# A weight column in 12 to 14 vector operations instead of 17, and another order of the opening work of a group-norm convolution

## The chip, the cores and the metric

One core of one Trainium2 chip. The metric is device time in microseconds (us) of one execution; medians of several executions are quoted, with the lowest and the highest. A traced execution also has a span, which is some 1.7 us shorter than its time (1101.58 against 1099.8 in the one traced run of the kernel before).

## The reference, cut to what matters

```python
x = x + conv(group_norm(x), quantise(U))       # x: 160 images of 128 channels, 32x32, fp32

# group norm: 32 groups of 4 channels; mean and variance over (4, 32, 32)
# the convolution: 5 weight sets, set n for images n*32 .. n*32+31 of the kernel's order;
#   3x3, 128 -> 128 channels, padding 1
s1 = (max(U) - min(U)) / 3                     # over ALL five sets
v1 = s1 * floor(U / s1)
s2 = s1 / 5
v2 = s2 * floor((U - v1) / s2)
w  = v1 + v2
```

Two things follow for the start. No weight can be quantised before all five sets have been read and reduced to one maximum and one minimum. And with k1 and k2 for the two floors, w = s2 * (5*k1 + k2): the bracket is a small integer, exact in half precision, so the kernel puts only the integers into TensorE's weights and multiplies s2 into the normalised image.

## The kernel before: the parts that matter

A column is one of the three columns of the 3x3 stencil: 128x128x3 weights, read with a stride of 3 elements. It takes seven VectorE instructions for each floor, and 17 in all:

```python
def floor_div(self, k, v, n, t, parts):
    r, nr, hi, lo = parts                     # 1/s, -1/s, s in two parts
    yield nc.vector.tensor_scalar(n, v, r, ROUND, ALU.mult, ALU.add)      # round by adding a
    yield nc.vector.tensor_scalar_add(n, n, -ROUND)                       # large constant
    yield nc.vector.scalar_tensor_tensor(t, n, hi, v, ALU.mult, ALU.subtract)
    yield nc.vector.scalar_tensor_tensor(t, n, lo, t, ALU.mult, ALU.add)
    yield nc.vector.scalar_tensor_tensor(t, t, nr, n, ALU.mult, ALU.add)
    yield nc.vector.tensor_tensor(t, t, n, ALU.is_lt)
    yield nc.vector.tensor_sub(k, n, t)

def quantise(self, pool, un, name, combine):
    ...
    yield from self.floor_div(k1, un, nn, tt, self.parts1)
    yield nc.vector.tensor_scalar_mul(v1, k1, self.s1)
    yield nc.vector.tensor_sub(rest, un, v1)
    yield from self.floor_div(k2, rest, nn, tt, self.parts2)
    yield combine(k1, k2, v1)                 # in make_column: m = 5*k1 + k2
```

`make_column` then transposes the column on TensorE and takes it out of PSUM (TensorE's result memory) on ScalarE (`wt`). Each image is normalised by ScalarE (`z`) and split into a half-precision high part (`hi`, ScalarE) and a low part (`lo`, VectorE). Images 0 to 2 are convolved directly: for each column six 128x512 products with the high part and six with the low part, accumulated in PSUM. From image 3 on the low part goes through combined rows (`conv`, with `d` and `st`).

In the traces here every engine's instructions come in the order in which the program issues them (e3 below moves one small product, and what stood behind it starts 5.9 us sooner), so the text below is read as the order of the work on each engine. The opening:

```python
chain = self.steps.from_range(spread)         # s1, s2, reciprocals, shrink: small VectorE steps
column = self.make_column(0, 1)
...                                           # chain and column 1 interleaved
measure(0, 1)                                 # sums and squares of images 0, 1 on ScalarE
self.stats[0].means(); self.stats[0].deviations(); self.stats[0].variances()
measure(2, 3)
self.stats[0].scales()
self.stats[1].means()
self.normalise(0); self.high_part(0)
self.stats[1].deviations(); self.stats[1].variances()
self.normalise(1); self.high_part(1)
self.stats[1].scales()
run(column)                                   # transposes, wt
self.low_part(0); self.low_part(1)
self.normalise(2); self.high_part(2)
self.normalise(3); self.high_part(3)
self.conv_direct(0, 1); self.conv_direct(1, 1)
column = self.make_column(0, 0)               # the second column: begun here
take(column, 5); self.low_part(2); measure(4, 5)
run(column); measure(6, 7)
self.conv_direct(2, 1); self.conv_direct(0, 0)
self.stats[2].means(); self.stats[2].deviations()
...
run(self.make_column(0, 2))                   # the third column
for i in range(self.imgs):
    for st in ready: st.means()               # small TensorE products for images 8 and up,
    for st in middle: st.variances()          # ahead of image i's products
    if i < self.FIRST: self.conv_direct(i, 2) # FIRST = 3
    else: self.conv(i)
    ...
```

A group's statistics take a chain over the engines: sums (ScalarE), `mv` (POOL), `means` (a small product on TensorE over the four channels), `ngm` (ScalarE), `dv` (POOL), `variances` (TensorE), `ve` (copied by ScalarE, then worked on by POOL with `shrink`), `rstd` and `shift` (POOL), and only then `z`.

## Time and profile before

| | value |
|---|---|
| time | 1100.32 us median of 3 (1100.0 to 1101.24) |
| span of the traced run (1101.58 us) | 1099.8 us |
| first product of image 0 | 34.41 us |
| first product of image 3 | 74.07 us |
| first product of image 4 | 83.55 us |
| image 4 to the end | 1016.25 us |

From image 4 on TensorE never waits, so the whole question is what happens in the first 84 us. The prediction below shows the lines. To read them: a line of the timeline gives start, duration, engine, line of the program, operation, operands; the bracket at its end is the engine's idle time before it and what ended that. A wait line gives total us, times, longest.

One more line matters when two traces are compared. VectorE reduces the weights as they arrive, and the first of the 128x1152 reductions waits for a transfer; from there eight of them run without a gap and the scales follow. Before:

```profile
7.42 1.35 DVE L381 TENSOR_REDUCE ext<-u 128x1 f32<-128x1152 f32 x1 [0.89 <-DMA u<-in_L_conv_U_dram]
```

This moment differs from trace to trace (6.98 to 8.89 us in the nine of this study) with the landing of that transfer; the kernels e3 and e4, which are alike up to image 3, have it at 8.21 and 7.57. Where I write "from the landing", times are counted from it.

### The profile page before, as it was taken

How to read it: one execution, taken by the hardware profiler on the slowest of the kernel's cores; microseconds unless marked ns; L12 is line 12 of the kernel's file. 1: busy time of each engine (PE TensorE's matmuls, PEld its weight loads, DVE VectorE, ACT ScalarE, POOL GpSimd, SP SyncE). 2: the span in 40 equal slices, each digit the busy share in tenths (PEclk: the TensorE clock that was granted, in tenths of full speed). 3: DMA queues.
4: the chain of work that ended last, by engine and by line, in shares of the span. 5: the costliest groups of instructions: out<-in, count | busy, mean ns of one | idle time of the engine just before them, and what ended most of it. 6: DMA issues, size and time to landing. Idle time of an engine off the chain costs nothing.

```text
span 1099.8 us, 16007 instructions
## 1 busy us (share of the span) xinstructions
PE 1051.8 (96%) x5901; PEld 577.6 (53%) x5901; DVE 903.9 (82%) x1518; ACT 772.9 (70%) x1043; POOL 389.4 (35%) x716
## 2 busy tenths in 40 slices
PE   1689999999999999999999999999999999999997
PEld 0235555555555555555555555555555555555554
DVE  7868998897797989878889897797989877777774
ACT  4767977768776777777777768776778777776541
POOL 3423443342334343424353443334343423232210
PEclk9889999999999999999999999999999999999999
DMA  9506889889897989998979988888999898985664
GB/s 360 205 1 182 231 227 257 250 233 249 229 260 200 262 255 259 243 262 228 264 191 283 252 240 243 232 238 222 246 274 261 231 246 232 254 231 144 169 165 159
DMA packets 65462, 252.05 MB, mean 229 GB/s; under 512 B 3936, under 2 KB 3936, under 8 KB 65376
## 3 DMA queue, kind: packets, MB, share of 16 engines
q1 hardware_dynamic: 43344, 170.73, 42.1%
q0 software_dynamic: 22032, 80.23, 38.9%
q8 instruction: 48, 0.79, 0.3%
q14 instruction: 38, 0.31, 0.1%
HBM read 86.84 MB, written 83.89 MB: 155 GB/s over the span
## 4 chain that ended last, share of the span: by engine, by line
PE 94%; DVE 3%; DMA 1%; POOL 0%; ACT 0%; issue 0%; SPq 0%; DVEq 0%
PE eo L499 55%; PE eo L526 19%; PE m L526 19%; PE m L499 1%; DMA u<-in_L_conv_U_dram 1%; DVE ext L381 0%; DVE ext L382 0%; DVE xt L588 0%; DVE lo L465 0%; PE pg L211 0%; PE pt L415 0%; ACT z L452 0%; PE pg L196 0%; ACT hi L460 0%; POOL rstd L219 0%
## 5 line engine op out<-in xcount | busy, mean ns | idle before, releaser
L499 PE MATMUL eo<-hi,wt 128*128 128x512 f16 (+1 forms) x2862 | 686.8, 376 | 1.2 <-ACT wt L417 1.2
L499 PEld LDWEIGHTS <-wt 128*128 128x128 f16 x2934 | 288.7, 99 | 278.2 <-issue 8.3
L526 PEld LDWEIGHTS <-wt 128*128 128x128 f16 x2826 | 276.9, 99 | 196.0 <-issue 3.7
L552 ACT ACTIVATE mm<-m 128x1024 f16<-128x1024 f32 x157 | 160.0, 1019 | 233.4 <-PE m L526 233.4
L526 PE MATMUL eo<-d,wt 128*128 128x256 f16 (+1 forms) x1884 | 283.7, 273 | 0.0
L526 PE MATMUL m<-st,wt 128*128 128x512 f16 x942 | 230.4, 381 | 1.9 <-DVE xt L588 1.9
L452 ACT ACTIVATE z<-xt,shift,rstd 128x1024 f32<-128x1024 f32 x160 | 197.6, 1235 | 37.9 <-POOL shift L222 37.9
L465 DVE TENSOR_TENSOR lo<-z,hi 128x1024 f16<-128x1024 f32 x160 | 194.6, 1217 | 8.6 <-ACT hi L460 8.4
L581 DVE SCALAR_TENSOR_TENSOR sum<-pq,eo 128x1024 f32<-128x1024 f16 x153 | 185.9, 1215 | 16.0 <-PE eo L526 15.8
L190 POOL TENSOR_SCALAR mv<-squares 128x1 f32<-128x1 f32 x122 | 67.4, 553 | 313.8 <-ACT junk L187 311.3
L561 DVE TENSOR_TENSOR pq<-mm 128x512 f16<-128x512 f16 x157 | 66.4, 423 | 133.5 <-ACT mm L552 132.3
L594 POOL DMA_DIRECT2D xt<-sum x153 | 136.6, 894 | 85.4 <-DVE sum L581 69.5
L460 ACT CAST hi<-z 128x1024 f16<-128x1024 f32 x160 | 166.0, 1037 | 0.1
L187 ACT ACTIVATE junk<-xt,minus 128x1024 f16<-128x1024 f32 x122 | 140.5, 1152 | 2.5 <-POOL minus L180 1.5
L178 ACT ACTIVATE junk<-xt 128x1024 f16<-128x1024 f32 x122 | 127.7, 1047 | 11.3 <-DMA xt<-in_x_dram 11.1
L479 DVE TENSOR_TENSOR d<-lo 128x1024 f16<-128x1024 f16 x157 | 109.1, 695 | 5.4
L180 POOL TENSOR_SCALAR minus<-total 128x1 f32<-128x1 f32 x122 | 42.0, 345 | 107.1 <-ACT junk L178 106.3
L481 DVE TENSOR_TENSOR st<-lo 128x512 f16<-128x512 f16 x157 | 65.7, 419 | 0.0
L562 DVE TENSOR_TENSOR pq<-mm 128x512 f16<-128x512 f16 x157 | 65.5, 417 | 0.0
L482 DVE TENSOR_TENSOR st<-lo 128x512 f16<-128x512 f16 x157 | 65.4, 417 | 0.0
L171 DVE BATCH_NORM_STATS2 st<-xt 128x6 f32<-128x512 f32 x76 | 48.6, 680 | 0.0
L181 POOL TENSOR_SCALAR mv<-total 128x1 f32<-128x1 f32 x122 | 44.4, 364 | 0.1
(88 smaller groups left out, 416.1 us busy)
## 6 DMA issues: line engine op xcount, KB each, us to landing
xt<-in_x_dram SPq DMA_DIRECT2D x39, 2048.0 KB, 13.5
out_dram<-xt SPq DMA_DIRECT2D x39, 2048.0 KB, 7.4
xt<-sum POOLq DMA_DIRECT2D x153, 512.0 KB, 8.0
u<-in_L_conv_U_dram SPq DMA_DIRECT2D x4, 576.0 KB, 7.2
xt<-in_x_dram SPq DMA_DIRECT2D x4, 512.0 KB, 9.7
out_dram<-xt SPq DMA_DIRECT2D x3, 512.0 KB, 3.1
u<-in_L_conv_U_dram SPq DMA_DIRECT2D x2, 288.0 KB, 3.1
out_dram<-xt SPq DMA_DIRECT2D x2, 256.0 KB, 4.0
```

The source lines that it names most:

```text
L178: nc.scalar.activation(junk, image, ACTF.Copy, accum_out=total)
L187: nc.scalar.activation(junk, image, ACTF.Square, bias=self.minus[j], accum_out=squares)
L190: nc.gpsimd.tensor_scalar_mul(self.mv[:, j, 1:2], squares, 1.0 / image.shape[1])
L452: nc.scalar.activation(z, self.image(i), ACTF.Identity, bias=st.shift[:, j : j + 1], scale=st.rstd[:, j : j + 1],)
L460: self.nc.scalar.copy(hi.rearrange("p h w -> p (h w)"), self.z[i])
L465: self.nc.vector.tensor_sub(lo[:, 1 : self.H + 1, :].rearrange("p h w -> p (h w)"), self.z.pop(i), self.hi[i].rearrange("p h w -> p (h w)"),)
L479: nc.vector.tensor_sub(d, lo[:, 0:H, :], lo[:, 2 : H + 2, :])
L499: nc.tensor.matmul(target[:, h, r0 - h0 : r1 - h0, c0:c1], self.wts[n, col][:, k, :], tile[:, s0 : s0 + r1 - r0, c0 + dw : c1 + dw], start ...
L526: nc.tensor.matmul(target[:, :, c0:c1], self.wts[n, col][:, kind, :], source[:, :, c0 + dw : c1 + dw], start=start, stop=stop,)
L552: self.nc.scalar.mul(m, self.m.pop(i).rearrange("p a i w -> p a (i w)"), UP)
L581: nc.vector.scalar_tensor_tensor(self.sum[i], self.m.pop(i), 0.5 / UP, eo, ALU.mult, ALU.add)
L594: self.nc.gpsimd.dma_start(self.image(i), self.sum.pop(i), accum_op=ALU.add)
```

## The change

The intent: shorten what VectorE has to do for a column, and reorder the opening so that no engine waits for what another could have done earlier. A column takes 13 VectorE instructions, 12 where ScalarE does the first rounding (the second and third column), and 14 from image set 1 on. Cut to its core:

```diff
+    def nearest(self, pool, v, parts, name, by_scalar=False):
+        dt = mybir.dt.int16 if by_scalar else I32       # a conversion in place of ROUND
+        engine = self.nc.scalar.mul if by_scalar else self.nc.vector.tensor_scalar_mul
+        engine(n, v, parts[0])
     def floor_div(...):
-        yield nc.vector.tensor_scalar(n, v, r, ROUND, ALU.mult, ALU.add)
-        yield nc.vector.tensor_scalar_add(n, n, -ROUND)
-        yield nc.vector.scalar_tensor_tensor(t, n, hi, v, ALU.mult, ALU.subtract)
+        yield nc.vector.scalar_tensor_tensor(t, n, hi, v, ALU.mult, ALU.add)   # hi, lo of -s
     def quantise(...):
-        yield nc.vector.tensor_scalar_mul(v1, k1, self.s1)
-        yield nc.vector.tensor_sub(rest, un, v1)
+        yield nc.vector.scalar_tensor_tensor(rest, k1, self.parts1[1], un, ALU.mult, ALU.add)
     def make_column(self, n, col, by_scalar=False):
-        ... m = k1 * 5 + k2 on VectorE, 3 transposes
+        if n == 0: parts = ((k1, self.ident5), (k2, self.ident))     # merged on TensorE:
+        else: (m as before) parts = ((m, self.ident),)               # 5*I and I, in fp32 PSUM
@@ the opening @@
+        measure(0, 0, 1); measure(1, 0, 1)              # measure(stage, *images)
+        self.stats[0].means(); self.stats[0].deviations()
+        measure(0, 2, 3)
+        self.stats[0].variances(); self.stats[0].scales()
+        take(second, 1)                                 # ScalarE rounds the second column
+        measure(1, 2, 3)
+        self.stats[1].means(); self.stats[1].deviations()
+        parts(0)                                        # z and hi of image 0
+        self.stats[1].variances(); self.stats[1].scales()
+        self.normalise(1)
+        run(first)                                      # transposes, wt of the first column
+        self.high_part(1); parts(2)
+        take(second, 2); self.low_part(0)               # second column between the low parts
+        take(second, 2); self.low_part(1)
+        take(second, 2); self.low_part(2)
+        for part in (self.direct_hi, self.direct_lo):   # high parts of all three, then low
+            for i in range(self.FIRST): part(i, self.COLS[0])
+        measure(0, 4, 5); take(third, 1); measure(1, 4); run(second); measure(1, 5)
+        parts(3); measure(0, 6, 7)
+        ...                                             # products of the second column
+        run(third); measure(1, 6, 7); self.low_part(3); self.combinations(3)
@@ the loop, i < 3 @@
-                self.conv_direct(i, 2)
+                j = (i - 1) % self.FIRST                # the third column: images 2, 0, 1
+                self.direct_hi(j, self.COLS[2]); self.direct_lo(j, self.COLS[2])
+                (at i = 0 the means and deviations, at i = 1 the variances and scales of group 2)
+                self.residual(j)
```

More of the change, by code (lines that the diff above doesn't have):

```diff
@@ L31 @@
 WIDEST = 40.0
-ROUND = 12582912.0
 class Steps:
@@ L42, in __init__ @@
         self.parts1, self.parts2 = (
-            tuple(self.col(tag + part) for part in ("r", "nr", "hi", "lo"))
+            tuple(self.col(tag + part) for part in ("r", "n", "nhi", "nlo"))
             for tag in ("s1", "s2")
@@ L64, in parts @@
         def parts(out, s):
-            r, nr, hi, lo = out
+            r, neg, hi, lo = out
             yield nc.vector.reciprocal(r, s)
+            yield nc.vector.tensor_scalar_mul(neg, s, -1.0)
             yield nc.vector.tensor_single_scalar(
-                hi.bitcast(I32), s.bitcast(I32), -4096, op=ALU.bitwise_and
+                hi.bitcast(I32), neg.bitcast(I32), -4096, op=ALU.bitwise_and
             )
-            yield nc.vector.tensor_sub(lo, s, hi)
-            yield nc.vector.tensor_scalar_mul(nr, r, -1.0)
+            yield nc.vector.tensor_sub(lo, neg, hi)
         span = col("span")
@@ L97, in choose @@
         nc.vector.tensor_copy(self.far, far)
+    def nearest(self, pool, v, parts, name, by_scalar=False):
+        tag = "ns" if by_scalar else "nn"
+        dt = mybir.dt.int16 if by_scalar else I32
+        n = pool.tile(list(v.shape), dt, tag=tag, name=f"{tag}_{name}")
+        engine = self.nc.scalar.mul if by_scalar else self.nc.vector.tensor_scalar_mul
+        engine(n, v, parts[0])
+        return n
     def floor_div(self, k, v, n, t, parts):
         nc = self.nc
-        r, nr, hi, lo = parts
@@ L105, in floor_div @@
-        yield nc.vector.tensor_scalar(n, v, r, ROUND, ALU.mult, ALU.add)
-        yield nc.vector.tensor_scalar_add(n, n, -ROUND)
-        yield nc.vector.scalar_tensor_tensor(t, n, hi, v, ALU.mult, ALU.subtract)
+        r, _, hi, lo = parts
+        yield nc.vector.scalar_tensor_tensor(t, n, hi, v, ALU.mult, ALU.add)
         yield nc.vector.scalar_tensor_tensor(t, n, lo, t, ALU.mult, ALU.add)
-        yield nc.vector.scalar_tensor_tensor(t, t, nr, n, ALU.mult, ALU.add)
+        yield nc.vector.scalar_tensor_tensor(t, t, r, n, ALU.mult, ALU.add)
@@ L110, in floor_div, with quantise @@
         yield nc.vector.tensor_tensor(t, t, n, ALU.is_lt)
         yield nc.vector.tensor_sub(k, n, t)
-    def quantise(self, pool, un, name, combine):
-        nc = self.nc
-        nn, tt, k1, k2, v1, rest = (
-            pool.tile(list(un.shape), F32, tag=tag, name=f"{tag}_{name}")
-            for tag in ("nn", "tt", "k1", "k2", "v1", "rest")
+    def quantise(self, pool, un, name, dt, by_scalar=False):
+        yield (nn := self.nearest(pool, un, self.parts1, name, by_scalar))
+        tt, k1, k2, rest = (
+            pool.tile(list(un.shape), kind, tag=tag, name=f"{tag}_{name}")
+            for tag, kind in (("tt", F32), ("k1", dt), ("k2", dt), ("rest", F32))
@@ L120, in quantise @@
         )
         yield from self.floor_div(k1, un, nn, tt, self.parts1)
-        yield nc.vector.tensor_scalar_mul(v1, k1, self.s1)
-        yield nc.vector.tensor_sub(rest, un, v1)
+        yield self.nc.vector.scalar_tensor_tensor(
+            rest, k1, self.parts1[1], un, ALU.mult, ALU.add
+        )
+        yield (nn := self.nearest(pool, rest, self.parts2, name + "_2"))
         yield from self.floor_div(k2, rest, nn, tt, self.parts2)
-        yield combine(k1, k2, v1)
+        return k1, k2
@@ L128, in run @@
 def run(steps):
-    for _ in steps:
-        pass
+    while True:
+        try:
+            next(steps)
+        except StopIteration as end:
+            return end.value
 def group_mean_matrix(nc, pool):
@@ L247, in general_path @@
             wn = one.tile([P, C, TAPS], F32, tag="w", name=f"g_w{n}")
-            def combine(k1, k2, v1, wn=wn):
-                return nc.vector.scalar_tensor_tensor(
-                    wn, k2, steps.s2, v1, ALU.mult, ALU.add
-                )
-            run(steps.quantise(one, un, f"g{n}", combine))
+            k1, k2 = run(steps.quantise(one, un, f"g{n}", F32))
+            nc.vector.tensor_scalar_mul(wn, k1, steps.s1)
+            nc.vector.scalar_tensor_tensor(wn, k2, steps.s2, wn, ALU.mult, ALU.add)
             wt = one.tile([P, TAPS, C], F32, tag="wt", name=f"g_wt{n}")
@@ L399, in over_partitions, with make_column @@
         return spread
-    def make_column(self, n, col):
+    def make_column(self, n, col, by_scalar=False):
         nc, P = self.nc, self.P
-        m = self.qpool.tile([P, P, ROW], MM, tag="m", name=f"m{n}_{col}")
-        def combine(k1, k2, v1):
-            return nc.vector.scalar_tensor_tensor(m, k1, 5.0, k2, ALU.mult, ALU.add)
         un = self.us[n].rearrange("o i (r c) -> o i r c", c=ROW)[:, :, :, col]
-        yield from self.steps.quantise(self.qpool, un, f"{n}_{col}", combine)
-        pt = self.ps_tr.tile([P, ROW, P], MM, tag="pt", name=f"pt{n}_{col}")
-        for k in range(ROW):
-            nc.tensor.transpose(pt[:, k, :], m[:, :, k], self.ident)
+        k1, k2 = yield from self.steps.quantise(self.qpool, un, f"{n}_{col}", MM, by_scalar)
+        if n == 0:
+            parts = ((k1, self.ident5), (k2, self.ident))
+        else:
+            m = self.qpool.tile([P, P, ROW], MM, tag="m", name=f"m{n}_{col}")
+            yield nc.vector.scalar_tensor_tensor(m, k1, 5.0, k2, ALU.mult, ALU.add)
+            parts = ((m, self.ident),)
+        pt = self.ps_tr.tile([P, ROW, P], F32, tag="pt", name=f"pt{n}_{col}")
+        for k in range(ROW):
+            for j, (part, diagonal) in enumerate(parts):
+                nc.tensor.matmul(
+                    pt[:, k, :], part[:, :, k], diagonal,
+                    start=(j == 0), stop=(j == len(parts) - 1),
+                )
         wt = self.wpool.tile([P, 6, P], MM, tag=f"wt{col}", name=f"wt{n}_{col}")
@@ L508, in banks, with direct_hi @@
         return pool.tile([self.P, 2, self.H // 2, self.W], F32, tag=tag, name=f"{tag}{i}")
-    def conv_direct(self, i, col):
+    def direct_hi(self, i, col):
         if i not in self.eo:
@@ L514, in conv_direct, with direct_lo @@
         self.taps(i, (self.hi[i], 0), col, self.eo[i], False)
+    def direct_lo(self, i, col):
         lo = self.los[i % len(self.los)]
@@ L621, in run @@
         nc.gpsimd.tensor_copy(self.ident, ident)
+        self.ident5 = self.const.tile([P, P], MM, tag="ident5", name="ident5")
+        nc.gpsimd.tensor_scalar_mul(self.ident5, ident, 5.0)
         self.gavg = group_mean_matrix(nc, self.const)
@@ L626, in run @@
         self.los = []
-        for k in range(3):
+        for k in range(4):
             lo = self.const.tile([P, self.H + 2, self.W], MM, tag=f"lo{k}", name=f"lo{k}")
@@ L638, in take, with measure @@
                 next(steps, None)
-        def measure(*images):
-            for stage in (0, 1):
-                for i in images:
-                    self.measure(i, (stage,))
-        chain = self.steps.from_range(spread)
-        column = self.make_column(0, 1)
-        take(chain, 6)
-        take(column, 1)
-        take(chain, 1)
-        take(column, 1)
-        take(chain, 2)
-        take(column, 1)
-        for _ in range(7):
-            take(chain, 1)
-            take(column, 1)
+        def measure(stage, *images):
+            for i in images:
+                self.measure(i, (stage,))
@@ L658, in run, with parts @@
+        def parts(i):
+            self.normalise(i)
+            self.high_part(i)
+        chain = self.steps.from_range(spread)
+        first, second, third = (
+            self.make_column(0, col, by_scalar=col != self.COLS[0]) for col in self.COLS
+        )
+        for ahead in (6, 2, 1, 1, 1, 1, 1, 2, 2, 1):
+            take(chain, ahead)
+            take(first, 1)
         run(chain)
-        measure(0, 1)
+        measure(0, 0, 1)
+        measure(1, 0, 1)
         self.stats[0].means()
@@ L661, in run @@
         self.stats[0].deviations()
+        measure(0, 2, 3)
         self.stats[0].variances()
-        measure(2, 3)
         self.stats[0].scales()
+        take(second, 1)
+        measure(1, 2, 3)
         self.stats[1].means()
-        self.normalise(0)
-        self.high_part(0)
         self.stats[1].deviations()
+        parts(0)
         self.stats[1].variances()
+        self.stats[1].scales()
         self.normalise(1)
+        run(first)
         self.high_part(1)
-        self.stats[1].scales()
@@ L673, in run @@
-        run(column)
+        parts(2)
+        take(second, 2)
         self.low_part(0)
+        take(second, 2)
         self.low_part(1)
-        self.normalise(2)
-        self.high_part(2)
-        self.normalise(3)
-        self.high_part(3)
-        self.conv_direct(0, 1)
-        self.conv_direct(1, 1)
-        column = self.make_column(0, 0)
-        take(column, 5)
-        self.low_part(2)
-        measure(4, 5)
-        run(column)
-        measure(6, 7)
-        self.conv_direct(2, 1)
@@ L689, in run @@
-        self.conv_direct(0, 0)
-        self.stats[2].means()
-        self.stats[2].deviations()
-        self.conv_direct(1, 0)
-        self.stats[2].variances()
-        self.stats[2].scales()
-        self.conv_direct(2, 0)
-        run(self.make_column(0, 2))
+        take(second, 2)
+        self.low_part(2)
+        for part in (self.direct_hi, self.direct_lo):
+            for i in range(self.FIRST):
+                part(i, self.COLS[0])
+        measure(0, 4, 5)
+        take(third, 1)
@@ L697, in run @@
+        measure(1, 4)
+        run(second)
+        measure(1, 5)
+        parts(3)
+        measure(0, 6, 7)
+        for i in range(self.FIRST):
+            self.direct_hi(i, self.COLS[1])
+            self.direct_lo(i, self.COLS[1])
+        run(third)
+        measure(1, 6, 7)
+        self.low_part(3)
+        self.combinations(3)
         self.steps.choose()
@@ L707, in run @@
             if i < self.FIRST:
-                self.conv_direct(i, 2)
+                j = (i - 1) % self.FIRST
+                self.direct_hi(j, self.COLS[2])
+                self.direct_lo(j, self.COLS[2])
+                if i == 0:
+                    self.stats[2].means()
+                    self.stats[2].deviations()
+                elif i == 1:
+                    self.stats[2].variances()
+                    self.stats[2].scales()
+                self.residual(j)
             else:
@@ L722, in run @@
                 self.high_part(i + 3)
-            if self.FIRST <= i + 2 < self.imgs:
+            if self.FIRST < i + 2 < self.imgs:
                 self.low_part(i + 2)
                 self.combinations(i + 2)
-            if i < self.FIRST:
-                self.residual(i)
-            elif i > self.FIRST:
+            if i > self.FIRST:
                 self.residual(i - 1)
```

## The prediction

> **What bounds the kernel now.** I read the busy table first, then TensorE's waits, then busy times by stretch with the cuts laid where TensorE starts and stops, then the timeline of the first 92 us.
>
> ```profile
> PE 1051.8 (96%) x5901; PEld 577.6 (53%) x5901; DVE 903.9 (82%) x1518; ACT 772.9 (70%) x1043; POOL 389.4 (35%) x716
> ```
>
> 96% busy says where to look, not that TensorE is the limit everywhere. The stretches (start:end, length, then busy us and instructions of PE, PEld, DVE, ACT, POOL, then granted clock, DMA share, GB/s) divide the span:
>
> ```profile
> 0.00:34.40 34.40, 3.76 (x15) 2.77 (x15) 26.75 (x54) 16.38 (x28) 12.55 (x36) 1.00 0.95 371
> ...
> 42.00:46.80 4.80, 0.03 (x1) 0.04 (x2) 4.44 (x10) 3.43 (x6) 2.04 (x6) 0.91 0.00 0
> ...
> 69.00:74.07 5.07, 0.40 (x3) 0.32 (x3) 5.04 (x8) 4.85 (x7) 1.28 (x3) 0.91 0.00 0
> 74.07:83.55 9.48, 9.48 (x39) 4.46 (x38) 7.06 (x13) 4.20 (x6) 1.53 (x5) 0.69 0.00 0
> 83.55:1093.00 1009.45, 1008.95 (x5731) 557.39 (x5729) 838.55 (x1397) 724.75 (x966) 359.10 (x637) 1.00 0.85 234
> ```
>
> From 83.55 us, the first product of image 4, TensorE is busy for 1008.95 of 1009.45 us at full clock, and in that stretch the waits view lists none for it. So the end is 83.55 us plus a constant, and the change can only move the 83.55. Ahead of it TensorE waits, and works at a reduced clock after long waits. Its waits:
>
> ```profile
> PE pg L211 <- POOL dv L208: 6.9, 1, 6.9
> PE pt L415 <- DVE m L409: 4.8, 1, 4.8
> ...
> PE pg L196 <- POOL mv L181: 2.7, 1, 2.7
> PE m L526 <- DVE xt L588: 1.9, 1, 1.9
> ```
>
> The first direct product waits for statistics, not for the column of weights; the second column (4.8) is late because VectorE makes it; then image 3 waits for the sum of image 11 (2.7) and for the residual add that empties its PSUM banks (1.9). The timeline gives the moments:
>
> ```profile
> 26.56 0.15 DVE L82 SCALAR_TENSOR_TENSOR shrink<-s2r 128x1 f32<-128x1 f32 x1
> ...
> 28.59 1.24 ACT L452 ACTIVATE z<-xt,shift,rstd 128x1024 f32<-128x1024 f32 x1 [3.32 <-POOL shift L222]
> ...
> 30.22 0.56 DVE L409 SCALAR_TENSOR_TENSOR m<-k,k 128x384 f16<-128x384 f32 x1
> ...
> 34.41 2.69 PE L499 MATMUL eo<-hi,wt 128*128 128x512 f16 x6 [0.58 <-ACT wt L417]
> ...
> 64.03 1.23 ACT L452 ACTIVATE z<-xt,shift,rstd 128x1024 f32<-128x1024 f32 x1
> ...
> 71.49 0.20 POOL L181 TENSOR_SCALAR mv<-total 128x1 f32<-128x1 f32 x1
> ...
> 71.75 0.39 PE L196 MATMUL pg<-mv,gavg 128*128 128x4 f32 x2 [2.74 <-POOL mv L181]
> ...
> 74.07 2.72 PE L526 MATMUL m<-st,wt 128*128 128x512 f16 x6 [1.94 <-DVE xt L588]
> ```
>
> **What the Trainium skill says.** (1) "TensorE: Matmul & The Clock Gate", Part 1 (the HAM clock gate): an idle window of about 3.4 us halves the clock, and a busy one restores it. The trace agrees: after 4.8 us without work six products take 2.5 us apart (47.07 to 49.57), warm 1.27; after waits of 0.6 us they stay warm. (2) "VectorE: DVE Perf Modes", the perf-mode tier table: in fp32 a tensor-scalar runs two elements a cycle, a tensor-tensor one. The trace: 0.36 us (constants) or 0.42 (pointer) against 0.56 on 128x384; scalar-tensor-tensor with a pointer 0.62, with the strided weights 0.73. (3) "ScalarE: Activation LUTs", What ACT_TABLE_LOAD costs: 186 ns plus 0.833 ns an element, 93 ns more per pointer operand; the 128x1024 cast here takes 1.037 us against 1.039 by that. For the new 128x384 scaling with a pointer it gives an estimate of 0.60 us. (4) "GPSIMD Engine Reference", Key points: it shares SBUF interfaces with VectorE. Here a POOL add on two elements took 1.24 us beside a VectorE subtraction, 0.20 otherwise, so POOL steps carry some tenths of doubt.
>
> **The change, part by part.** *A column.* Rounding by adding and taking off a large constant (two instructions) becomes one conversion to an integer, twice a column; the two instructions for k1*s1 and u minus it become one; for image set 0 the merge into m goes to TensorE (six small products in place of three transposes). On VectorE that leaves 13, and 12 where ScalarE does the first rounding. Twelve by the rows, in order: 0.73 + 0.62 + 0.62 + 0.56 + 0.56 + 0.73 (the difference to u, strided) + 0.42 + 0.62 + 0.62 + 0.62 + 0.56 + 0.56 = 7.22, plus 0.04 between dependent ones = 7.7 us, against 10.2 for the 17 of the old third column (46.63 to 56.83). From image set 1 on it is 14 in place of 17, in the stretch where TensorE never waits: worth nothing.
>
> *First stretch, VectorE.* With the old spacing (0.04 us between dependent large ones, small ones in the gaps) from the reciprocal at 20.61, the new order puts the shrink factor at 26.93 to 27.08 (before 26.56: the negated scale lies ahead of its high part) and the last k at 29.53 (m before: 30.78). The old chain from the end of the column operations at 26.78 to z of image 0 is 1.81 us; so z0 starts at 28.89, 0.3 later. But ScalarE now reads the second pair's mean before z0 instead of behind its high part (30.82 before), so the second pair's deviations are summed at about 30.2 to 30.7 instead of 32.9, and the transposes follow, done by 31.7. Then in ScalarE's order: z0 28.89, high part 0 +1.27, copy +0.98, z1 +0.09, weights +1.15 = 32.4; first product +0.54 (old 33.86 to 34.40) = **32.9, 1.5 earlier** than 34.41.
>
> *Direct products.* High parts of three images come first, ready at 31.2, 34.1 and 36.4; low parts at 32.4, 35.4 and 37.9, each before its turn. 12 products cold take 4.83 us (old 34.41 to 39.24), 24 warm 4 x 1.27: 42.8. VectorE, second column between the low parts: done at 41.4, so the 4.8 us wait goes. Transposes, weights and first product: old 60.28 to 61.20 = 0.92, plus about 0.2 for three more: 44.0. 36 products: 6 x 1.27 = 7.6: 51.6. Third column on VectorE 41.4 + 7.7 = 49.1: no wait. Weights start on ScalarE at 52.2, products 52.8 to 60.7 with 0.3 for small statistics products. The old ones ended at 69.0: **8.3 earlier**, warm throughout.
>
> *Image 3.* It is not released by these. The matmul of the means of images 8 to 11 stands ahead of it on TensorE and needs image 11's sum, which ScalarE makes behind z4, z5 and others, and z4 needs the scales of images 4 to 7. In the new order two squares (6, 7), the mean, sum and square of image 9 and the variance copy stand behind the third weights. With old spacings: weights 0.54, square 1.33, square 1.40, mean 0.15, sum to square 1.69, square to copy 1.15, copy to z4 1.94 = 8.2, so z4 at 60.4 (64.03 before). From z4 to the means' matmul it was 7.72, of which 0.67 was a slow POOL step: 7.1 to 7.7, so 67.5 to 68.1, and image 3's products at about **68.0 instead of 74.07**: the residual add has its banks free before that. TensorE is idle from 60.7 to 68, so it starts cold again, as before; the stretch to image 4 stays 9.48 us. ScalarE must have z6 done before it empties image 3's banks: 60.4 + 9.9 = 70.3 against 70.7, just in time.
>
> Sum: 1.5 (earlier start) + 4.8 and a cold run of 2.9 (second column) minus small pieces = 8.3 on the direct products, of which 2.2 are lost in the longer wait for image 11's sum: 6.1 us. 1100.3 - 6.1 = 1094.2.
>
> **Rivals.** *TensorE never waits after 33 us*: image 3 starts at 60.8 and warm, a gain of 13.3 + 2.8 (9.48 against about 6.6 warm): 1084.2. For it: everything else is ready by then. Against it: the means' matmul stands before image 3 in TensorE's instruction order, and the 7.1 us of ScalarE work. *The second column stays late*, because VectorE waits for high parts between its instructions (it has three such waits): the old 4.8 us would return in part, up to 3 us, giving some 1097. My walk has 1.4 us to spare there. *ScalarE becomes the bound at image 4*: if z4 to z6 slips while image 3 doesn't, image 4 waits for the eviction, 1 to 2 us: 1096. For it: 0.4 us to spare. *The saved VectorE work counts in the steady part*: VectorE is 83% busy there, TensorE 100%; nothing.
>
> **Range and chances.** One cold run more or less ragged is +-1 us, POOL steps +-0.7, a wait overlooked 2 to 3 us, and the first rival's partial form (sums of image 11 sooner) 1 to 2 us on the good side. So 1091.5 to 1097.2. A gain over 2% is 22 us, more than all of TensorE's waits after 34.4 us (4.8 + 2.7 + 1.9 + 0.6 = 10.1) and its three cold runs (some 2.4 + 2.9 + 2.9) together: not to be had. A loss over 2% would need a new stall in every image.
>
> **What would show it.** Right: first direct product near 32.9, no wait for the second column, direct products over by 61, then one wait of about 7 us whose releaser is POOL's mean of image 11, image 3 near 68, image 4 near 77.5, then no TensorE waits. Wrong: the first product after 34 (step one); a wait before the second transposes; image 3 starting before 66 or after 70; TensorE waits after 80 us, which would mean that the integer or half-precision operands cost VectorE more than here.

## The result, and the profile after

Run beside the kernel before on one chip: before 1100.16 us (1098.88 to 1101.24, 4 runs), after **1095.34 us** (1094.96 to 1096.09, 4 runs). The ratio is **0.9958**, 95% interval 0.994 to 0.9975: a gain of 4.8 us that is real, but far under 2%. The result is right. The traced execution of the kernel before is slower than all four of these (1101.58 us) and that of the kernel after its fastest (1094.96), so the two traces lie 6.5 us apart (1099.8 and 1093.3) where the medians lie 4.8 apart; steps below are read from the traces.

| us | first product | direct products end | image 3 | image 4 | span |
|---|---|---|---|---|---|
| before | 34.41 | 69.0 | 74.07 | 83.55 | 1099.8 |
| after | 34.20 | 61.46 | 68.64 | 76.82 | 1093.3 |
| difference | -0.2 | -7.5 | -5.4 | -6.7 | -6.5 |

The busy table of the kernel after, to set against the prediction's first fence:

```profile
PE 1048.2 (96%) x5910; PEld 577.5 (53%) x5910; DVE 892.3 (82%) x1468; ACT 772.6 (71%) x1045; POOL 383.6 (35%) x718
```

VectorE lost 11.6 us of work. That is not where the time came from: the gain is won before image 4. Its stretches show it (start:end, length, then busy us of PE, PEld, DVE, ACT, POOL, granted clock, DMA share, GB/s):

```profile
61.46:68.19 6.73, 0.00 (x1) 0.00 (x1) 3.81 (x5) 6.73 (x10) 0.99 (x5) 0.77 0.00 0
68.64:76.82 8.18, 8.18 (x40) 4.05 (x40) 6.82 (x13) 6.44 (x9) 1.73 (x6) 0.80 0.00 0
76.82:1086.50 1009.68, 1009.38 (x5731) 557.76 (x5729) 832.46 (x1363) 723.86 (x966) 351.30 (x637) 1.00 0.85 234
```

After the direct products TensorE stands still for 6.73 us while ScalarE is busy for all of it; then image 3's products run at a granted clock (TensorE's mean clock in the stretch, 1.00 is full) of 0.80 and take 8.18 us, where they took 9.48 at 0.69 before; then 1009.4 us of work without a wait. From image 4 to the end is 1016.48 us (before 1016.25), although VectorE has 6.1 us less to do there. TensorE's waits after:

```profile
PE pg L223 <- POOL dv L220: 7.4, 1, 7.4
PE pg L208 <- POOL mv L193: 6.7, 1, 6.7
PE eo L513 <- ACT wt L431: 1.7, 2, 1.1
PE m L513 <- ACT wt L431: 0.6, 1, 0.6
```

The first line is the wait ahead of the first product, for the statistics of images 2 and 3; it was 6.9 us before. The wait for the second column (4.8 us before) is gone, and so is the one for the residual add (1.9). The one for POOL's mean of image 11 has grown from 2.7 to 6.7 us. From the timeline of the kernel after, the moments that the steps of the prediction named:

```profile
7.92 1.35 DVE L389 TENSOR_REDUCE ext<-u 128x1 f32<-128x1152 f32 x1 [1.38 <-DMA u<-in_L_conv_U_dram]
...
27.38 0.15 DVE L81 SCALAR_TENSOR_TENSOR shrink<-s2r 128x1 f32<-128x1 f32 x1
27.50 0.62 DVE L114 SCALAR_TENSOR_TENSOR tt<-nn,s2nlo,tt 128x384 f32<-128x384 int32 x1
27.71 0.54 POOL L229 TENSOR_SCALAR ve<-ve,shrink 128x2 f32<-128x2 f32 x1 [3.93 <-DVE shrink L81]
...
29.39 0.56 DVE L117 TENSOR_TENSOR k<-nn,tt 128x384 f16<-128x384 int32 x1
29.43 0.57 POOL L234 TENSOR_TENSOR shift<-ngm,rstd 128x2 f32<-128x2 f32 x1
30.04 1.24 ACT L466 ACTIVATE z<-xt,shift,rstd 128x1024 f32<-128x1024 f32 x1 [3.70 <-POOL shift L234]
...
34.20 4.48 PE L513 MATMUL eo<-hi,wt 128*128 128x512 f16 x12 [1.11 <-ACT wt L431]
...
42.22 0.56 DVE L117 TENSOR_TENSOR k<-nn,tt 128x384 f16<-128x384 int32 x1
...
43.59 0.50 PE L426 MATMUL pt<-ident,k 128*128 128x128 f16 x6
...
61.15 1.24 ACT L466 ACTIVATE z<-xt,shift,rstd 128x1024 f32<-128x1024 f32 x1 [2.06 <-POOL shift L234]
...
67.92 0.21 POOL L193 TENSOR_SCALAR mv<-total 128x1 f32<-128x1 f32 x1
...
68.19 0.59 PE L208 MATMUL pg<-mv,gavg 128*128 128x4 f32 x2 [6.73 <-POOL mv L193]
68.64 2.72 PE L542 MATMUL m<-st,wt 128*128 128x512 f16 x6
```

The second column's k is done at 42.78 us, 0.8 before TensorE comes to its transposes (43.59; they carry no bracket, so TensorE did not wait). Image 3 starts right behind two small products that had waited 6.73 us for POOL's mean.

The two POOL steps between `shrink` and `z` are the surprise. In the kernel before, the same steps on the same two elements were:

```profile
26.89 0.29 POOL L217 TENSOR_SCALAR ve<-ve,shrink 128x2 f32<-128x2 f32 x1 [1.37 <-DVE big L86]
...
28.36 0.20 POOL L222 TENSOR_TENSOR shift<-ngm,rstd 128x2 f32<-128x2 f32 x1
```

After, they take 0.54 and 0.57 us: each starts just behind a large VectorE instruction with two tensor inputs (L114 at 27.50, L117 at 29.39) and ends within 0.15 us of its end.

### The profile page after: what moved, and what is told of

It is laid out like the page before. It is cut to its first block, busy times and chain, and to the rows that moved or that the text cites. A ratio compares the mean times of both kernels' runs of the same rounds, so it can differ in the third digit from the quotient of the medians.

```text
span 1093.3 us, 15987 instructions
## 1 busy us (share of the span) xinstructions
PE 1048.2 (96%) x5910; PEld 577.5 (53%) x5910; DVE 892.3 (82%) x1468; ACT 772.6 (71%) x1045; POOL 383.6 (35%) x718
## 4 chain that ended last, share of the span: by engine, by line
PE 95%; DVE 2%; ACT 1%; DMA 1%; POOL 1%; issue 0%; SPq 0%; POOLq 0%
PE eo L513 56%; PE eo L542 19%; PE m L542 19%; PE m L513 1%; DMA u<-in_L_conv_U_dram 1%; DVE ext L389 0%; DVE ext L390 0%; ACT z L466 0%; PE pg L223 0%; PE pg L208 0%; ACT junk L190 0%; PE pt L426 0%; ACT junk L199 0%; POOL rstd L231 0%; ACT wt L431 0%
## 5 line engine op out<-in xcount | busy, mean ns | idle before, releaser
L202 POOL TENSOR_SCALAR mv<-squares 128x1 f32<-128x1 f32 x122 | 60.4, 496 | 302.3 <-ACT junk L199 299.4
L192 POOL TENSOR_SCALAR minus<-total 128x1 f32<-128x1 f32 x122 | 35.0, 287 | 122.6 <-ACT junk L190 122.1
L193 POOL TENSOR_SCALAR mv<-total 128x1 f32<-128x1 f32 x122 | 50.5, 414 | 0.0
```

## The experiments

Seven kernels ran, in two jobs: e1 to e4 in the first, e5 to e7 in the second. In the first job the kernel before took 1101.15 us (1099.16 to 1102.25, 11 runs), in the second 1101.02 (1099.13 to 1102.63, 9 runs). All seven gave the right result. The table has every kernel's milestones in its trace; "landing" is the moment described above.

| kernel | ratio to before, 95% | landing | first product | image 3 | image 4 | span |
|---|---|---|---|---|---|---|
| before | | 7.42 | 34.41 | 74.07 | 83.55 | 1099.8 |
| after | 0.9958, 0.994 to 0.9975 | 7.92 | 34.20 | 68.64 | 76.82 | 1093.3 |
| e1_short_column | 0.9988, 0.9975 to 1.0002 | 6.98 | 35.27 | 71.99 | 81.02 | 1097.6 |
| e2_new_order | 0.9973, 0.996 to 0.9986 | 8.89 | 35.23 | 72.36 | 80.72 | 1097.3 |
| e3_means_behind | 0.9914, 0.9901 to 0.9927 | 8.21 | 34.49 | 62.74 | 73.29 | 1092.2 |
| e4_image3_ahead | 0.9896, 0.9882 to 0.991 | 7.57 | 33.86 | 60.65 | 68.68 | 1086.1 |
| e5_weights_sooner | 0.9946, 0.9932 to 0.996 | 8.27 | 33.36 | 68.25 | 77.56 | 1094.1 |
| e6_all | 0.9874, 0.9858 to 0.9889 | 7.46 | 32.55 | 60.33 | 66.75 | 1086.0 |
| e7_after_again | 0.9955, 0.9941 to 0.9968 | 8.10 | 34.38 | 68.79 | 76.97 | 1093.5 |

Counting from the landing is sound: the first product comes 26.28 us after it in after, e3 and e7 and 26.29 in e4, which have the same start, though their landings lie 0.64 us apart.

### e1_short_column: the shorter column in the old order

The opening and the loop of the kernel before, put back into the changed kernel:

```diff
-        measure(0, 0, 1); measure(1, 0, 1)
-        ...                                    # the new opening
+        measure(0, 1)
+        ...                                    # the opening of the kernel before
-        take(second, 2); self.low_part(0)
-        take(second, 2); self.low_part(1)
-        take(second, 2); self.low_part(2)
+        self.conv_direct(0, 1); self.conv_direct(1, 1)
+        column = self.make_column(0, 0)        # 13 operations a column, all on VectorE
+        take(column, 4); self.low_part(2)
@@ the loop, i < 3 @@
-                j = (i - 1) % self.FIRST
-                ...
+                self.conv_direct(i, 2)
```

> The shorter column alone, in the order of the kernel before (13 vector instructions for all three columns of image set 0, 14 later). My theory: the second column is done about 2 us sooner, TensorE's wait for it falls from 4.8 to about 2.8 us, and image 3 and the end come 2 to 4 us sooner than before: 1096 to 1098 us. Rival (the whole gain is in the order): within 1 us of before, 1099.2 to 1101. Rival (the gain is in the column alone): as the changed kernel, near 1095.

Measured: 1099.63 us (1098.03 to 1101.65, 6 runs), 1.3 us under the kernel before by the ratio, with an interval that touches 1: by time alone the shorter column in the old order is not shown to gain anything, and it gained less than expected: the median lies in the range of the rival that the whole gain is in the order. The trace shows why. Its waits and image 3:

```profile
PE pt L426 <- DVE k L117: 3.0, 1, 3.0
```

```profile
71.99 2.72 PE L540 MATMUL m<-st,wt 128*128 128x512 f16 x6 [1.94 <-DVE xt L602]
```

The wait for the second column shrinks from 4.8 to 3.0 us, so the column is shorter as worked out. But the first product is later: 28.29 us after the landing against 26.99. `z` of image 0 starts 22.16 us after the landing (before 21.17, after 22.12): in the new column the shrink factor comes later and the POOL steps behind it are slow, in either order, and here that costs 1.0 us. The other 0.3 us lie at the transposes, six in place of three (0.80 us against 0.48). So the shorter column by itself wins at the second column and pays at the first.

### e2_new_order: the old column in the new order

```diff
-        (nearest, the 12- or 13-operation floor_div and quantise, the merge on TensorE)
+        (the 17-operation column of the kernel before; its intermediates share tiles to fit)
-        take(second, 2); self.low_part(0); ...
+        take(second, 3); self.low_part(0); ...
```

> The new order with the old 17-instruction column (its intermediates share tiles to fit; no rounding on ScalarE). My theory: the second column comes about 2 us and the third about 1 us too late for TensorE, which then waits for both; image 3 at about 71 to 72.5 us instead of 68.6; the end about 3 us behind the changed kernel: 1097.5 to 1099. Rival (the order alone does it): as the changed kernel, near 1095.3. Rival (the column alone does it): as before, near 1100.

Measured: 1098.53 us (1097.37 to 1098.98), ratio 0.9973, 3.0 us gained, as expected. Image 3 starts at 72.36 us, also as expected. Both later columns are now a little late (about 2 and 1 us had been expected; timeline):

```profile
45.92 0.35 PE L415 MATMUL pt<-ident,m 128*128 128x128 f16 x3 [1.31 <-DVE m L409]
...
56.18 0.35 PE L415 MATMUL pt<-ident,m 128*128 128x128 f16 x3 [1.55 <-DVE m L409]
```

So most of the gain is the order's; the shorter column takes away the 1.31 and the 1.55 us that the order leaves. By time the parts are 1.3 and 3.0 us and both together 4.6 to 5.0 (the two measurements of the changed kernel). From the landing to image 3 they are 1.6 and 3.2 us, both together 5.9: in the traces they help each other, because each alone still leaves a late column. By time the surplus is smaller than the intervals (some 1.3 us either way) and is not shown. The first product comes 26.34 us after the landing here and 26.28 in the changed kernel, so the 0.7 us gained at the start are the order's alone. The way to it differs, though. With the old column POOL's `ve` and `shift` take 0.29 and 0.20 us again, and `z` of image 0 starts 21.16 us after the landing, 0.96 sooner than in the changed kernel. That gains nothing, since ScalarE's copy of the second pair's variances, which stands ahead of `z` of image 1, waits for POOL's `mv` and `dv` steps: these take 2.71 us here, 1.70 in the changed kernel.

```profile
30.05 1.24 ACT L452 ACTIVATE z<-xt,shift,rstd 128x1024 f32<-128x1024 f32 x1 [3.30 <-POOL shift L222]
...
32.37 0.44 POOL L208 TENSOR_TENSOR dv<-dv,mv 128x2 f32<-128x2 f32 x1
...
33.49 0.16 ACT L216 COPY ve<-pg 128x2 f32<-128x2 f32 x1 [1.12 <-PE pg L211]
```

And from image 4 to the end this kernel, with 17 operations a column, takes 1016.58 us; the changed one takes 1016.48. The VectorE work saved in the steady part is worth nothing.

### e3_means_behind: is image 3 held by the small products alone?

My theory: nothing holds image 3 but the small product for images 8 to 11 that stands ahead of it. The rival: something else would be late as well (its combined rows, PSUM, ScalarE), so moving the small product gains little.

```diff
-            for st in ready: st.means()
-            for st in middle: st.variances()
+            first_group = i in (self.FIRST, self.FIRST + 1)
+            if not first_group:
+                (as before)
             ... self.conv(i)
+            if first_group:
+                for st in ready: st.means()
+                for st in middle: st.variances()
```

> Only the place of two small statistics products on TensorE changes: the means of images 8 to 11 behind image 3's products instead of ahead, the variances behind image 4's. My theory (image 3 is held by nothing else): it starts at 61.3 us, warm, right behind the direct products; image 4 is then held by the eviction of image 3's PSUM banks, which ScalarE reaches at about 71 us, so it starts at about 72 instead of 76.8; end 2 to 5 us sooner than the changed kernel, 1090.5 to 1093.5, the lower gain if image 4 starts cold. Rival (image 3 waits for something else too, such as its own operands or banks): image 3 stays after 65 us and the end within 1 us of the changed kernel.

Measured: 1092.18 us (1090.01 to 1093.88), ratio 0.9914, as expected; image 3 came at 62.74 us where 61.3 was expected, as the landing was 0.3 later and the first twelve products slower. In the timeline image 3 follows the direct products with no bracket:

```profile
62.74 1.46 PE L542 MATMUL m<-st,wt 128*128 128x512 f16 x6
...
73.29 1.49 PE L542 MATMUL m<-st,wt 128*128 128x512 f16 x6 [3.27 <-ACT mm L568]
```

That settles it for image 3: 5.9 us sooner than in the changed kernel, and nothing else held it. But image 4 now waits 3.3 us for ScalarE to empty image 3's banks (`mm`), because that eviction stands behind other work in ScalarE's order, and after that wait its products run at a clock of 0.79. The end moves by some 3 us by the medians, 4.5 to 4.8 by the ratios, not by 6.

### e4_image3_ahead: and the eviction moved as well

As e3, with image 3's products and the eviction of its banks issued one turn of the loop earlier:

```diff
             if i < self.FIRST:
                 ...
                 self.residual(j)
+                if i == self.FIRST - 1:
+                    self.conv(self.FIRST)
+                    self.leave(self.FIRST)
-            else:
+            elif i > self.FIRST:
                 self.conv(i)
...
-            if i >= self.FIRST:
+            if i > self.FIRST:
                 self.leave(i)
```

> As the run with the means behind, and the products and the eviction of image 3 are issued one image earlier, so that ScalarE empties its banks behind image 10's square, at about 66 us, not behind z6. My theory: no wait over 2 us is left after the direct products; image 3 at 61.3, image 4 at 68 to 70 (held by image 11's sum), all warm; end 6 to 8.5 us sooner than the changed kernel: 1087 to 1089.5. Rival (ScalarE is the true bound of this stretch and takes its time back at images 5 to 7): new TensorE waits there, and an end no better than the run with the means behind, 1091 or more.

Measured: 1089.5 us (1087.82 to 1089.98, 4 runs), ratio 0.9896, at the upper end of what was expected. Timeline:

```profile
60.65 1.46 PE L542 MATMUL m<-st,wt 128*128 128x512 f16 x6
...
68.44 0.39 PE L208 MATMUL pg<-mv,gavg 128*128 128x4 f32 x2 [1.20 <-POOL mv L193]
68.68 1.46 PE L542 MATMUL m<-st,wt 128*128 128x512 f16 x6
```

Six products in 1.46 us at both images: TensorE stays at full clock where the changed kernel's six took 2.72. Two waits are left after the direct products, 1.2 us for the same mean of image 11 and 0.5 us for VectorE at image 5. Image 3 comes 1.45 us sooner from the landing than in e3; up to there the two kernels are alike, so that is chance. All four runs are under all five of e3, by as little as 0.03 us. This version beats both kernels: its slowest run (1089.98) is under the changed kernel's fastest (1094.96).

### e5_weights_sooner: is the gain of an earlier first product passed on?

The changed kernel, with POOL summing the second pair's deviations before it waits for the shrink factor, and ScalarE taking the weights out of PSUM ahead of `z` of image 1:

```diff
-        self.stats[0].scales()
+        self.stats[0].copy_variances()
         take(second, 1)
         measure(1, 2, 3)
         self.stats[1].means()
         self.stats[1].deviations()
-        parts(0)
         self.stats[1].variances()
+        self.stats[0].finish_scales()
         self.stats[1].scales()
-        self.normalise(1)
+        parts(0)
         run(first)
-        self.high_part(1)
+        parts(1)
```

> The changed kernel with two moves at the very start: POOL sums the second pair's deviations before it waits for the shrink factor, and ScalarE turns the first weights out of PSUM behind the high part of image 0, ahead of the normalisation of image 1. My theory: the first direct product starts 1.2 to 1.4 us sooner (32.9 against 34.2 us when the weights land as in the first look); VectorE's second column then comes about 0.5 us too late for TensorE, and what is left, 0.6 to 1.0 us, is passed on to image 3 and the end: 0.5 to 1.2 us under the changed kernel. Rival (the first product's start is hidden by the wait for image 11's sum, 6.7 us): image 3 and the end don't move.

Measured: 1095.21 us (1094.15 to 1096.08), ratio 0.9946, beside 0.9955 for the changed kernel in the same job: by time no difference, where 0.5 to 1.2 us had been expected. In the timeline the first product is 25.09 us after the landing in place of 26.28, and image 3 comes 59.98 after it in place of 60.72, so 0.7 of the 1.2 us are passed on. Of the rest, 0.43 us is a new wait for the high part of image 2, which had not been expected. In this trace the 0.7 are then lost:

```profile
33.36 4.16 PE L519 MATMUL eo<-hi,wt 128*128 128x512 f16 x12 [2.29 <-ACT wt L437]
```

```profile
68.25:77.56 9.31, 9.31 (x39) 4.42 (x40) 7.24 (x13) 6.44 (x9) 1.19 (x6) 0.70 0.00 0
```

Image 3's products, the same work as in the changed kernel (8.18 us at a clock of 0.80), took 9.31 us at 0.70. From the landing, image 4 is 0.4 us later than in the changed kernel. The half-clock run after a long wait has no fixed length in these traces, and in this one it ate the gain; that it did so in the other four executions is not shown.

### e6_all: everything together

e4's loop and e5's start; besides, the means of images 8 to 11 stand between the two halves of image 4's products:

```diff
+    def conv(self, i, between=()):
         ...                                   # six products into m
+        for st in between: st.means()
         eo = ...                              # the other products
```

> Image 3 and its eviction ahead, as run before, with the start of the run with the weights sooner, and the means of images 8 to 11 between the first and second half of image 4's products, so that they hold nothing. My theory: 0.6 to 1.0 us from the start and 0.5 to 1.2 us from the wait for the sum before image 4; image 4 at about 66.5 us against 68.7 (weights landing as before), no TensorE wait over 1 us after the first product; end 1 to 2 us under the run with image 3 ahead, about 0.988 of before, 1086.5 to 1088.5. Rival (another wait takes its place, at images 5 to 7, on ScalarE or VectorE): no better than the run with image 3 ahead.

Measured: 1087.3 us (1086.56 to 1087.74, 4 runs), ratio 0.9874. The fastest of all, but its interval overlaps e4's, so it is not shown to be better. Its timeline says why so little is left:

```profile
66.75 1.46 PE L548 MATMUL m<-st,wt 128*128 128x512 f16 x6
...
75.10 1.46 PE L548 MATMUL m<-st,wt 128*128 128x512 f16 x6 [1.33 <-ACT mm L576]
```

From the landing, image 4 comes 1.8 us sooner than in e4 (59.29 against 61.11), image 5 only 0.2 (67.64 against 67.85): it waits 1.33 us for ScalarE's eviction of image 4. The rival, that another wait takes the place of the one removed, is right here.

### e7_after_again: the changed kernel once more

> The changed kernel unaltered, for comparison on this chip: 0.4% under before, 1094 to 1097 us; in the trace image 3 at about 68.6 us and image 4 at about 77, moved by as much as the third set of weights lands sooner or later than in the first look (first reduction on it at 7.9 us).

Measured: 1095.2 us (1095.09 to 1097.06), ratio 0.9955; image 3 at 68.79 and image 4 at 76.97. The changed kernel repeats its time and its trace, with a landing 0.18 us later.

## Why the prediction was right

It said 1094.2 (1091.5 to 1097.2), within 2%; measured 1095.34. The mechanism held for the later columns, for image 3 and for the steady part; the start of the first product was mis-sized, and it hangs on one chain more than the sum had. A second size was off in the other direction, which is luck for the total.

1. **The column.** 7.7 us for twelve operations; the third column on VectorE took 8.0 (42.88 to 50.87). Right. The rows used for fp32 also hold for the mixed operands: conversion to int32 0.42 to 0.48 us, scalar-tensor-tensor with an int32 operand 0.62, the last subtraction to half precision 0.56. Three of the twelve took 0.04 to 0.11 us more.

2. **The first product, "1.5 earlier": wrong in size.** It came at 34.20, not 32.9; "after 34" was the prediction's own sign against this step. Half a microsecond of the miss is chance: the landing was 0.50 later (7.92 against 7.42). The failed term is "the old chain from the end of the column operations at 26.78 to z of image 0 is 1.81 us" (the column operations are the small 128x1 ones). From the end of `shrink` (27.53) to z0 (30.04) it was 2.51. The two POOL steps account for 0.62 of the 0.70: 0.25 on `ve`, 0.37 on `shift`. The old figure came from a place where VectorE's instructions happened to lie otherwise; the new column's lie across both steps, and in e2, with the old column, both are fast. The prediction had named the cause and allowed "some tenths of doubt" for it, but left it out of the sum. The Trainium skill, "SBUF — State Buffer", Who interferes with whom, bears on this: a VectorE instruction with two inputs in SBUF contends with a POOL instruction that reads SBUF, and the section calls the ports that they share an exclusive lock. The trace agrees in shape (29.43 to 30.00 beside VectorE's 29.39 to 29.95). From the landing the first product is 0.7 us sooner, and by e2 that is the order's doing. Whether the 0.62 us are really lost at the first product no run shows: in e2 `z` of image 0 is not late and the first product is no sooner. The step that the sum left out is the second chain, that of the second pair's deviations, "summed at about 30.2 to 30.7". POOL had them at 31.79, because their steps stand behind `shift`; their product on TensorE ended at 32.43 and the high part of image 0 on ScalarE at 32.36, so two chains of the same length lead to the first product.

3. **The direct products, "the 4.8 us wait goes": right.** No wait for the second column, 0.8 us to spare (1.4 foreseen; VectorE came 1.4 us later than foreseen and TensorE 0.8); none for the third. They took 27.3 us from first to last product against 27.8 foreseen and ended at 61.46 against 60.7.

4. **Image 3 "is not released by these": right.** One wait of 6.73 us, released by POOL's mean of image 11; z4 at 61.15 (60.4 foreseen), from there to the small products 7.04 (7.1 to 7.7 foreseen), image 3 at 68.64 (68.0 foreseen). e3 proves the reading: with the small products moved, image 3 starts with no wait at all. Of the 7.5 us won on the direct products 2.1 went into this wait.

5. **"The stretch to image 4 stays 9.48 us": wrong in size.** It took 8.18, in e7 as well; image 4 came at 76.82, before the foreseen 77.5. The late start of image 3 (0.64) and this shorter stretch (1.3) partly cancel: that the total came within 1.1 us is in part luck. In the other kernels that have the same long wait, or the two of before, the stretch took 8.36 (e2), 9.03 (e1) and 9.31 (e5): its length is not a constant to be carried over. The work in it is: length times granted clock is 6.5 us in each of them (9.48 x 0.69, 9.31 x 0.70, 9.03 x 0.72, 8.36 x 0.78, 8.18 x 0.80).

6. **The steady part, "nothing": right.** TensorE lists no wait there, and image 4 to the end is 1016.25 to 1016.58 us in all six kernels that reach image 4 without moved products (before, after, e1, e2, e5, e7), old column or new.

The rivals: *TensorE never waits after 33 us* was wrong for the change, and e4 comes near it when the order allows it (waits of 1.2 and 0.5 us are left). *The second column stays late* happened in e1 and e2, where only half of the change is made. *ScalarE becomes the bound at image 4* was wrong for the change but right for e3, and in e6 for image 5.

What stays open: the traces' difference (6.5 us) is larger than the medians' (4.8). The landing differs by 0.18 us between the two traces of the changed kernel, and the half-clock run differs where the work is the same: after, e7, e3 and e4 are alike up to the end of the direct products, which took 27.3, 27.2, 28.3 and 26.8 us from the first one. A single trace of each kernel can't say how much of the 1.7 us is due to which. Why the stretch of image 3 was shorter than before, twice by the same 1.3 us, is open too.

## What to carry to other kernels

Saved vector work pays only where a later engine stands waiting for it: here 6.1 us of it in the steady part bought nothing, and at the start only together with an order that used it. When TensorE waits in front of a large piece of work, look at what it is really waiting for: a four-column product that nobody needs yet can hold back some forty large ones, because TensorE took them in the order of issue here (e3), and moving it, with the eviction that would otherwise wait next, was worth more than the whole change. Expect each removed wait to be paid back in part by the next one (7.5 us became 5.4), and a removed long wait to be worth its cold run (at half clock) too: here six products took 2.33 us after a wait of 2.99 (e1), but 1.45 after one of 1.55 (e2).

## What the Trainium skill lacked or had wrong

- "TensorE: Matmul & The Clock Gate", Part 1: it says that the window is free-running and the count of cold products varies, and advises not to fit one. The runs add how much that can be at one place. Four kernels that are alike up to there took 26.8 to 28.3 us for the direct products, and the same stretch of image 3, after 5 to 7 us without large products, took 8.18 (twice in one kernel), 8.36, 9.03, 9.31 and 9.48 us. In the one trace of e5 such a difference swallowed the gain; a difference of that size between two single traces is no result.
- "SBUF — State Buffer", Who interferes with whom: the lock agrees with the trace, but the page has no figure for what it does to tiny POOL steps on a path. Here a step on two elements went from 0.20 to 0.57 us beside a 0.56 us VectorE subtraction, and to 1.24 beside one of 1.23 us (the prediction's `dv`).
- "ScalarE: Activation LUTs", What ACT_TABLE_LOAD costs: its formula gave an estimate of 0.60 us for the new rounding pass of 128x384 with a pointer. It took 0.81:

```profile
23.01 0.81 ACT L104 ACTIVATE ns<-u,s1r 128x384 int16<-128x384 f32 x1
```

  The source is strided by 3 elements and the output is int16; no run tells the two apart.
- "VectorE: DVE Perf Modes", the perf-mode tier table: it has columns for bf16, fp32 and PSUM, and nothing on integer outputs or on scalar-tensor-tensor. Here a tensor-scalar from fp32 to int32 takes the 0.42 us of one from fp32 to fp32 (128x384, pointer), and scalar-tensor-tensor with one int32 operand takes 0.62 us, as with fp32 alone.
